# Moving the product that gives a routing position, and its copy, ahead of other work in an attention and mixture-of-experts block

## The chip, the cores and the metric

The kernel runs on one core of a Trainium2 chip. The core has five engines with queues of their own: TensorE (PE, matrix products; its weight loads are shown apart as PEld), VectorE (DVE), ScalarE (ACT), GpSimd (POOL) and SyncE (SP, which here only issues DMAs). Each engine works through its instructions in order and waits on semaphores for the others. The metric is the time of the program on the device in microseconds (us), the median of several runs. Everything is computed in float32.

## The reference

Input x has 4 sequences of 2048 tokens with 256 features, and N = 8192 tokens in all. A conditioning vector gives per sequence six vectors: shift, scale and gate for each of two halves.

```python
h = layernorm(x) * (1 + ca) + sa
x = x + ga * linear_attention(h)      # 16 heads of 16, causal
h = layernorm(x) * (1 + cb) + sb
x = x + gb * moe(h)                   # 8 experts, top 2
```

The attention is linear: queries and keys go through elu(.) + 1, a state S += k v^T runs along the tokens, and each output is (S q) / (z q) with z the running sum of keys. The mixture of experts works with a capacity:

```python
gates = softmax(h @ w_router.T)
topk_gates, topk_idx = top_k(gates, 2)
position_in_expert = cumsum(one_hot(topk_idx).sum(1), axis=0) - 1
keep = position_in_expert < 1280      # ceil(8192 / 8 * 1.25)
y = sum over the kept experts of gate * (silu(h @ w_gate.T) @ w_down[e].T)
```

So a token's place in an expert depends on all the tokens before it.

## The kernel before

Tokens are taken in 16 groups of G = 512, each of four tiles of 128 tokens. A first stage does the attention and the routing of all groups, a second stage (`expert`, line 667) does the eight experts, each on 1280 rows fetched from a table `slots` in DRAM.

In the first stage PE, ACT, DVE and POOL run exactly the order in which the program writes its instructions; nothing reorders them. The main loop (line 767) goes over steps `g` of four parts `j`, and weaves the work of five groups together: the attention of group `g` itself (`scores`, `attend`, `keep_state`, `from_state`, `project_out`), queries, values and denominators of group `nxt` = g+1, the first LayerNorm of `nrm` = g+2, second LayerNorm and router of `prv` = g-1, and the last routing part, `positions` and `dispatch`, of `old` = g-2. Loading is two groups ahead of that. So `positions` is called in 16 steps, g = 2 to 17, of which 13 also have values to compute.

These names are needed to follow the steps, with the lines of the profile:

- `project_out` (L504, L505): `pw` on PE, then DVE adds it to `x`, and the statistics follow (L285).
- `keys_by_token` (L366, L371): `pk` on PE, copied by ACT to `kk`.
- `running_keys` (L381, L386): a DVE scan `zc`, then a POOL product `qs`.
- `values` (L346, L354): `pv` on PE in two halves, each copied by ACT to `vpad` in two copies.
- `normalise` (L306): four ACT scalings, to `xna` for the first LayerNorm and to `hrow` for the second. `second_norm` (L516, L517) has POOL first fill columns of `hrow` with the sequence's modulation (four copies, only in steps with g%4 of 1 or 2).
- `positions` (L582, L585, L589): two products into one bank `pp`, a running count within the group (`tri` times `mask`) and the counts before it (`ones` times `cnt`), 128x32 each, then an ACT copy to `pos`. `mask` and `cnt` come from `ranks` (L566, L575) one step earlier.
- `dispatch` (L604 to L626): 14 small DVE operations from `pos` to the slot numbers `idx`, and the gate weights in `hrow`. The rows themselves are sent by POOL's indirect DMAs (`send`, L641) in parts j=2 and j=3.
- `scores` (L430, L436): `psc` on PE, and two DVE operations that mask it into `at`. `denominators` (L394, L399, L401): `pd` on PE, `den` and `rden` on DVE. `to_features` (L318, L319): four transposes `pta` or `ptm` on PE, an ACT scaling to `hTa` or `hTm`, twice each. `scaled_q` (L412, L417, L419): `pr` on PE, then DVE and ACT.
- `keep_state` (L451, L460, L461, L463): `pst` on PE, `s_add` on ACT, `s_acc` and `s_msk` on POOL.

PSUM has 8 banks. Four hold `psc`, one each `po` and `pst`, and only two are left for all tiles taken with `bank(...)`: `pk`, `pw`, `pv`, `pp`, `pd`, `pta`, `ptm`, `pr`, `pl`, `lt`, `pq`. A tile that takes one of the two banks has to wait until the tile before it in the same bank has been read. Which of the two a tile gets is decided when the program is built.

Of the kernel before, what the change touches and what calls it, by code (L numbers as in the profile page):

```python
# [66 lines left out]
def adaln_block(ctx: ExitStack, tc, x, wqkvT, woutT, wrT, wgT, wdT, cT, wmod, out):  # L67
# [8 lines left out]
    def bank(name):  # L76
        return ps.tile([P, 512], F32, tag="bank", name=name)
# [5 lines left out]
    def load_x(g):  # L83
        xs[g] = xpool.tile([P, NT, D], F32, tag="x", name=f"x_{g}")
        nc.sync.dma_start(xs[g], xg[g])
# [169 lines left out]
    def sums(g):  # L255

        xn = G_["xna", g] = w1.tile([P, NT, D], F32, tag="xna", name=f"xna_{g}")
        sm = small.tile([P, NT], F32, tag="suma", name=f"suma_{g}")
        for j in range(NT):
            nc.scalar.activation(xn[:, j, :], xs[g][:, j, :], AF.Identity, accum_out=sm[:, j : j + 1])  # L260
        nm = small.tile([P, NT], F32, tag="nma", name=f"nma_{g}")
        nc.gpsimd.tensor_scalar(nm, sm, -1.0 / D, None, ALU.mult)
        G_["nm"] = nm

    def squares(g):

        xn, nm = G_["xna", g], G_.pop("nm")
        sq = small.tile([P, NT], F32, tag="sqa", name=f"sqa_{g}")
        for j in range(NT):
            nc.scalar.activation(  # L270
                xn[:, j, :], xs[g][:, j, :], AF.Square, bias=nm[:, j : j + 1], accum_out=sq[:, j : j + 1]
            )
        ve = small.tile([P, NT], F32, tag="vea", name=f"vea_{g}")
        nc.gpsimd.tensor_scalar(ve, sq, 1.0 / D, LN_EPS, ALU.mult, ALU.add)
        rstd = small.tile([P, NT], F32, tag="rstda", name=f"rstda_{g}")
        nc.gpsimd.tensor_tensor(rstd, ve, mhalf, ALU.pow)
        nmr = small.tile([P, NT], F32, tag="nmra", name=f"nmra_{g}")
        nc.gpsimd.tensor_tensor(nmr, nm, rstd, ALU.mult)
        G_["ns", "a"] = nmr, rstd
# [22 lines left out]
    def normalise(g, which, src, dst):  # L302

        nmr, rstd = G_.pop(("ns", which))
        for j in range(NT):
            nc.scalar.activation(  # L306
                dst[:, j, :], src[:, j, :], AF.Identity, bias=nmr[:, j : j + 1], scale=rstd[:, j : j + 1]
            )

    def to_features(g, which, m):  # L310

        b = g // GPB
        xn = G_.pop(("xna", g)) if which == "a" else hrows[g % 2]
        hT = w1.tile([P, NH, G], F32, tag=f"hT{which}", name=f"hT{which}_{g}")
        for h in range(NH):
            pt = bank(f"pt{which}_{g}_{h}")
            for j in range(NT):
                nc.tensor.transpose(pt[:, j * P : (j + 1) * P], xn[:, j, h * P : (h + 1) * P], ident)  # L318
            nc.scalar.activation(  # L319
                hT[:, h, :], pt, AF.Identity,  # L320
                bias=modc[:, m, h, b : b + 1], scale=modc[:, m + 1, h, b : b + 1],
            )
        G_[f"hT{which}", g] = hT
# [255 lines left out]
    def positions(g):  # L579
        gt_, mask, rank, cnt = G_["route", g]  # L580
        pp = G_["pp"] = bank(f"pp_{g}")
        nc.tensor.matmul(  # L582
            pp[:, : NT * NE], tri, mask.rearrange("p j e -> p (j e)"), start=True, stop=False
        )
        nc.tensor.matmul(  # L585
            pp[:, : NT * NE], ones, cnt[:, :NT, :].rearrange("p j e -> p (j e)"), start=False, stop=True
        )
        pos = small.tile([P, NT * NE], F32, tag="pos", name=f"pos_{g}")
        nc.scalar.copy(pos, pp[:, : NT * NE])  # L589
        G_["pos"] = pos  # L590
# [38 lines left out]
    def free_slots(i, then):  # L629

        for e in range(NE):
            at = e * CAP + i * P
            init = nc.sync.dma_start(slots[at : at + P, :], free)
            apart(init, "to_slots", join=False)
            after(init, [then])
# [104 lines left out]
    with tc.manual_schedule(engines={ET.PE, ET.Activation, ET.DVE, ET.Pool}):  # L740
        for g in range(2):
            sums(g)
            squares(g)
            normalise(g, "a", xs[g], G_["xna", g])
            to_features(g, "a", 0)
            for h in range(NH):
                first_k = project(g, "k", h, D, 2)
            if g == 0:
                load_x(2)
                for i in range(2):  # L750
                    free_slots(i, first_k)
                for h in range(NH):
                    project(0, "q", h, 0, 1)
                running_keys(0, (0, 1))
                values(0, 0)
                values(0, 2)
                denominators(0)
                keys_by_token(0)
                scaled_q(0)
                gated_out(0)  # L760
            else:
                for i in range(2, 4):
                    free_slots(i, first_k)
        sums(2)

        last = None
        for s in range((NG + 2) * NT):
            g, j = divmod(s, NT)
            nxt = g + 1 if g + 1 < NG else None
            nrm = g + 2 if g + 2 < NG else None  # L770
            far = g + 3 if g + 3 < NG else None
            prv = g - 1 if 0 <= g - 1 < NG else None
            old = g - 2 if g >= 2 else None

            def done(last=last):
                if last is not None:
                    project_out(*last)
                    if last[1] == NT - 1:
                        added.append(nc.sync.dma_start(og[last[0]], xs[last[0]]))

            if g < NG:
                masked = scores(g, j)
                if s % 2 == 1 and 4 + s // 2 < TPE:
                    free_slots(4 + s // 2, masked)
            if last is not None:
                attend(*last)
            if nxt is not None and j == 2:
                denominators(nxt)
            if prv is not None and j == 3:
                logits(prv)  # L790
            if g < NG and not (g % GPB == GPB - 1 and j == NT - 1):
                keep_state(g, j)
            for i in {2: (0, 1), 3: (2, 3)}.get(j, ()):
                if old is not None:
                    send(old, i)
            if j == 0:
                if nxt is not None:
                    project(nxt, "q", 0, 0, 1)
                done()
                if prv is not None:  # L800
                    spread_of(prv)
                if nxt is not None:
                    project(nxt, "q", 1, 0, 1)
                    running_keys(nxt, (0,))
                if nrm is not None:
                    squares(nrm)
            elif j == 1:
                if nxt is not None:
                    keys_by_token(nxt)
                done()  # L810
                if nxt is not None:
                    running_keys(nxt, (1,))
                    values(nxt, 0)
                    values(nxt, 2)
                if nrm is not None:
                    normalise(nrm, "a", xs[nrm], G_["xna", nrm])
                if prv is not None:
                    second_norm(prv)
                if old is not None:
                    positions(old)  # L820
                    dispatch(old)
                if far is not None:
                    load_x(far)
            elif j == 2:
                if nrm is not None:
                    to_features(nrm, "a", 0)
                done()
                if prv is not None:
                    to_features(prv, "m", 2)
                if nxt is not None:  # L830
                    scaled_q(nxt)
            else:
                if nrm is not None:
                    project(nrm, "k", 0, D, 2)
                done()
                if nrm is not None:
                    project(nrm, "k", 1, D, 2)
                if g % GPB == GPB - 1 and g + 1 < NG:
                    gated_out(g // GPB + 1)
                if far is not None:  # L840
                    sums(far)
                if prv is not None:
                    ranks(prv)
            last = None
            if g < NG:
                from_state(g, j)
                G_["s_old"] = G_.get("s_new")
                last = (g, j)
# [51 lines left out]
```

## Time and profile before

| | us |
|---|---|
| median of 9 runs | 1149.13 (1144.88 to 1158.18) |
| the profiled execution | 1149.41 |
| its span in the profile | 1147.7 |
| from one `pos` copy to the next in the middle of the loop (263.35 to 307.75) | 44.4 |
| first `pos` copy, last `pos` copy | 168.9, 781.0 |

Busy time over the span: PE 945.3 (82%), DVE 621.6 (54%), POOL 560.0 (49%), ACT 441.9 (39%). PE is busy longest, but this share is an average, and the granted TensorE clock moves between full and half speed during the run (mean 0.899).

A line of the timeline has the start in us from the span's start, the duration in us, the engine, the line of the kernel, the operation, output and inputs, shapes, how many instructions are merged into it, and in brackets the idle time of the engine just before with what ended it. A line of the waits has who waited for whom, total us, how many times, and the longest. A line of the stretches has the stretch, its length, the busy time of the engines with the number of records, the granted clock, the DMA share and GB/s.

### The profile page before, as it was taken

How to read it: one execution, taken by the hardware profiler on the slowest of the kernel's cores; microseconds unless marked ns; L12 is line 12 of the kernel's file. 1: busy time of each engine (PE TensorE's matmuls, PEld its weight loads, DVE VectorE, ACT ScalarE, POOL GpSimd, SP SyncE). 2: the span in 40 equal slices, each digit the busy share in tenths (PEclk: the TensorE clock that was granted, in tenths of full speed). 3: DMA queues.
4: the chain of work that ended last, by engine and by line, in shares of the span. 5: the costliest groups of instructions: out<-in, count | busy, mean ns of one | idle time of the engine just before them, and what ended most of it. 6: DMA issues, size and time to landing. Idle time of an engine off the chain costs nothing. (4 is left out here: it accounts for less than half of the span.)

```text
span 1147.7 us, 18139 instructions
## 1 busy us (share of the span) xinstructions
PE 945.3 (82%) x6832; PEld 668.7 (58%) x6832; DVE 621.6 (54%) x1244; ACT 441.9 (39%) x1054; POOL 560.0 (49%) x738
## 2 busy tenths in 40 slices
PE   6759988698898887888888988740899999888996
PEld 5437665465566666666656656520567556556664
DVE  3326566464764665665665566642655555544553
ACT  0456664455554545544545533210222222121221
POOL 3023561744645545645635646634535455454463
PEclk9889998798988989988988988875899999988998
DMA  5179977433232342331221110122665656555531
GB/s 183 49 271 387 369 300 258 157 122 127 101 144 93 112 167 93 112 134 68 76 101 70 46 48 29 45 77 79 258 227 189 217 199 217 180 189 180 199 120 55
DMA packets 71096, 173.61 MB, mean 151 GB/s; under 512 B 13664, under 2 KB 34400, under 8 KB 71008
## 3 DMA queue, kind: packets, MB, share of 16 engines
q1 hardware_dynamic: 39040, 101.66, 24.6%
q0 software_dynamic: 26112, 63.45, 15.0%
q10 hardware_dynamic: 5856, 7.35, 2.0%
q8 instruction: 53, 0.87, 0.3%
q14 instruction: 35, 0.29, 0.1%
HBM read 68.66 MB, written 129.20 MB: 172 GB/s over the span
## 5 line engine op out<-in xcount | busy, mean ns | idle before, releaser
L714 PE MATMUL pe<-wd,hid 128*128 128x256 f32 x640 | 162.5, 393 | 18.3 <-DVE y L721 8.1
L641 POOL DMA_INDIRECT slots<-hrow,idx x128 | 130.6, 1021 | 82.5 <-issue 34.0
L436 DVE TENSOR_TENSOR at<-psc,tri 128x1024 f32<-128x1024 f32 x128 | 150.1, 1214 | 28.5 <-PE psc L430 28.5
L714 PEld LDWEIGHTS pe<-wd,hid 128*128 128x128 f32 x640 | 118.4, 193 | 66.9 <-DVE y L721 25.6
L700 PE MATMUL ph<-hTe,wg_sb 128*128 128x512 f32 (+1 forms) x384 | 155.3, 530 | 1.2 <-ACT hTe L695 0.9
L726 POOL DMA_INDIRECT out_dram<-y,tok x80 | 84.1, 1051 | 104.5 <-issue 38.5
L708 ACT ACTIVATE th<-ph 128x512 f32<-128x512 f32 (+1 forms) x96 | 50.5, 526 | 196.6 <-PE ph L700 170.1
L675 POOL DMA_INDIRECT xc<-out_dram,tok x80 | 84.6, 1057 | 72.5 <-issue 43.0
L461 POOL TENSOR_TENSOR s_acc<-s_acc,s_add 128x256 f32<-128x256 f32 x56 | 45.7, 816 | 126.0 <-ACT s_add L460 119.8
L504 PE MATMUL pw<-wob,oT 128*128 128x256 f32 x256 | 79.5, 439 | 27.7 <-ACT hTa L319 11.5
L700 PEld LDWEIGHTS ph<-hTe,wg_sb 128*128 128x128 f32 x384 | 71.6, 193 | 43.7 <-issue 32.7
L709 DVE SCALAR_TENSOR_TENSOR hid<-th,ph 128x512 f32<-128x512 f32 (+1 forms) x96 | 57.2, 596 | 49.0 <-ACT th L708 40.2
L721 DVE SCALAR_TENSOR_TENSOR y<-pe,rows 128x256 f32<-128x256 f32 x80 | 38.6, 482 | 82.3 <-PE pe L714 61.4
L504 PEld LDWEIGHTS pw<-wob,oT 128*128 128x128 f32 x256 | 50.4, 209 | 53.3 <-issue 16.6
L483 PE MATMUL po<-at,vpad 128*32 128x128 f32 x2048 | 73.2, 276 | 3.5 <-issue 3.5
L430 PE MATMUL psc<-qeo,k 32*128 32x256 f32 x1024 | 75.2, 408 | 0.1
L483 PEld LDWEIGHTS po<-at,vpad 128*32 128x32 f32 x2048 | 54.0, 109 | 27.1 <-issue 26.7
L338 DVE SCALAR_TENSOR_TENSOR k<-exk,k 128x512 f32<-128x512 f32 x32 | 22.2, 692 | 87.1 <-ACT k L337 85.4
L332 PE MATMUL pk<-hTa,wqkv_sb 128*128 128x512 f32 x128 | 64.6, 631 | 4.4 <-ACT k L337 4.4
L318 PE MATMUL ptm<-ident,hrow 128*128 128x128 f32 x128 | 33.9, 412 | 39.7 <-DVE den L399 23.2
L332 PE MATMUL pq<-hTa,wqkv_sb 128*128 128x512 f32 x128 | 61.3, 604 | 5.1 <-ACT q L337 5.1
L346 PE MATMUL pv<-wqkv_sb,hTa 128*128 128x256 f32 x256 | 58.5, 382 | 0.0
(153 smaller groups left out, 1694.0 us busy)
## 6 DMA issues: line engine op xcount, KB each, us to landing
slots<-free SPq DMA_DIRECT2D x80, 518.0 KB, 6.8
rows<-slots SPq DMA_DIRECT2D x16, 2072.0 KB
rows<-slots SPq DMA_DIRECT2D x8, 1036.0 KB
x<-in_x_dram SPq DMA_DIRECT2D x16, 512.0 KB, 4.0
out_dram<-x SPq DMA_DIRECT2D x16, 512.0 KB, 6.4
wd<-in_wdT_dram ACTq DMA_DIRECT2D x8, 512.0 KB, 3.8
slots<-hrow,idx POOLq DMA_INDIRECT x128
wmod_sb<-in_wmod_dram ACTq DMA_DIRECT2D x1, 1536.0 KB
```

The costliest lines, as they stand in the source:

```text
L332: nc.tensor.matmul(pq, wqkv_sb[:, k, o + h * P : o + (h + 1) * P], hT[:, k, :], start=(k == 0), stop=(k == NH - 1))
L346: nc.tensor.matmul(pv[:, i * D : (i + 1) * D], hT[:, k, (j + i) * P : (j + i + 1) * P], wqkv_sb[:, k, 2 * D : 3 * D], start=(k == 0), stop ...
L430: nc.tensor.matmul(psc[:, a, h], kT[r : r + 32, h, cols], qeo[r : r + 32, h, :, cols], start=True, stop=True,)
L436: masked = nc.vector.tensor_tensor(at, psc[:, 2 * m : 2 * m + 2].rearrange("p i h q t -> p (i h q) t"), tri.unsqueeze(1).to_broadcast([P, ...
L483: nc.tensor.matmul(po[32 * a : 32 * a + 32, h * P : (h + 1) * P], vp[:, j, h * 4 + a, q : q + 2, :], att[a // 2][:, a % 2, h, q, :], start ...
L504: nc.tensor.matmul(pw[:, :D], oT[:, h, :], wob[:, h, :], start=(h == 0), stop=(h == NH - 1))
L641: row = nc.gpsimd.indirect_dma_start(out=slots[:, :], out_offset=bass.IndirectOffsetOnAxis(ap=idx[:, c, j : j + 1], axis=0), in_=hr[:, j, ...
L675: got = nc.gpsimd.indirect_dma_start(out=xc[:, i + j, :], out_offset=None, in_=out[:, :], in_offset=bass.IndirectOffsetOnAxis(ap=tok[:, j ...
L700: nc.tensor.matmul(ph[:, :m], wg_sb[:, k, f * P : (f + 1) * P], hT[:, k, :m], start=(k == 0), stop=(k == NH - 1),)
L709: nc.vector.scalar_tensor_tensor(hid[:, f, :m], th[:, :m], 1.0, ph[:, :m], ALU.add, ALU.mult)
L714: nc.tensor.matmul(pe[:, j, :], hid[:, f, j * P : (j + 1) * P], wds[e][:, f, :], start=(f == 0), stop=(f == NF - 1),)
L726: put = nc.gpsimd.indirect_dma_start(out=out[:, :], out_offset=bass.IndirectOffsetOnAxis(ap=tok[:, j : j + 1], axis=0), in_=y[:, j, :], in ...
```

## The change

In part j=1 of each step, `positions(old)` is called right after `done()` (which runs `project_out`), ahead of the second `running_keys`, the `values` of the next group and both LayerNorm scalings. `dispatch(old)` stays where it was. What is computed is unchanged.

```diff
                 if nxt is not None:
                     keys_by_token(nxt)
                 done()
+                if old is not None:
+                    positions(old)
                 if nxt is not None:
                     running_keys(nxt, (1,))
                     values(nxt, 0)
@@
                 if prv is not None:
                     second_norm(prv)
                 if old is not None:
-                    positions(old)
                     dispatch(old)
                 if far is not None:
                     load_x(far)
```

## The prediction

> **What bounds the kernel now.** I read the page first (span, clock), then the table of waits, then the timeline of one loop step, then stretches of the timeline against each other.
>
> ```profile
> span 1147.7 us, 18139 instructions
> ...
> DVE slot L604 <- ACT pos L589: 91.4, 16, 9.4
> ...
> PE ptm L318 <- DVE den L399: 23.2, 13, 4.3
> ```
>
> DVE's costliest wait is for `pos`: 16 times, 91.4 us. What matters is who queues behind it. The timeline of step g=8 shows that (start, duration, engine, line; in brackets the idle time before it and its releaser):
>
> ```profile
> 430.90 1.10 PE L504 MATMUL pw<-wob,oT 128*128 128x256 f32 x4 [0.57 <-ACT kk L371]
> ...
> 439.97 0.17 ACT L589 COPY pos<-pp 128x32 f32<-128x32 f32 x1
> ...
> 440.17 0.18 DVE L604 TENSOR_SCALAR slot<-pos 128x32 f32<-128x32 f32 x1 [6.00 <-ACT pos L589]
> 440.19 0.66 PE L318 MATMUL pta<-ident,xna 128*128 128x128 f32 x4 [0.68 <-ACT pos L589]
> ...
> 443.57 2.35 DVE L436 TENSOR_TENSOR at<-psc,tri 128x1024 f32<-128x1024 f32 x2
> ...
> 446.17 0.66 PE L318 MATMUL ptm<-ident,hrow 128*128 128x128 f32 x4 [1.80 <-DVE den L399]
> ```
>
> `pp` was done on PE at 435.82; its copy waited on ACT behind the value copies and eight scalings (436.02 to 440.06). DVE had been free since its scan ended at 434.17. Then 14 small `dispatch` operations (3.4 us), two masks and `den` ran in a row, and PE idled 0.68 + 0.87 + 0.87 + 1.80 + 0.87 = 5.1 us between `pst` and `pr`. The wait is on PE's path.
>
> A yardstick: step g=1 has the same work but no positions, dispatch or sends (stretch, length, PE busy, records, clock, DMA share, GB/s).
>
> ```profile
> 123.90:159.80 35.90, 33.62 (x345) 1.00 0.90 331
> 263.40:307.80 44.40, 38.02 (x349) 0.88 0.31 121
> ```
>
> 345 against 349 records (four are `pp`): 35.9 us at full clock, 44.4 us at 0.88. The clock, around the stall of g=9 (busy PE, PEld, DVE, ACT, POOL, then the clock):
>
> ```profile
> 482.30:485.70 3.40, 1.31 (x8) 0.84 (x8) 2.36 (x10) 2.44 (x7) 1.88 (x4) 1.00 0.40 108
> 485.70:489.10 3.40, 2.07 (x4) 1.17 (x4) 3.26 (x9) 0.24 (x1) 1.78 (x2) 0.50 0.26 96
> ```
>
> Of stretches of this length, laid on the clock's own steps, each at full clock with PE busy 49% or less is followed by half clock; one with 52% (441.3 to 444.7) is not. Half clock then lasts 10.2 us in nearly every step: `pr` takes 3.62 us there (g=10) and 2.05 in g=1.
>
> **The change part by part.** Nothing is added or removed: four `pp` matmuls and one copy move in each of 16 steps, 13 of which have values. DVE, POOL, SP and all DMAs keep their order.
>
> *PE.* `pp` now stands before the values. `cnt` (425.45) and its bank (freed by `kk`, 431.24) are long ready. As the program is built, `pp` and the first half of `pv` share a PSUM bank, so `pv` waits for the copy: it starts not at 431.84 but after 0.53 of `pp` (435.29 to 435.82), 0.17 of copy and twice 0.05 between engines, 0.8 later. `pp`'s old place gives back 0.2. Bounds: 0 (if later stalls hide it) and 0.8; I take 0.8, being nearest to g=1, which has no stall to hide it.
>
> *ACT.* `pos` costs 0.17 in either place. The rest of ACT is 0.8 late with `pv`: scalings end 440.86, `oT` and `s_add` follow, the first `hTa` ends 442.13 (was 441.66), the second 442.83 (was 443.19).
>
> *Banks.* The later banks change hands too: the second `pta` waits for `den` (as in g=1) and no longer for the first `hTa`; `pw` for the first `hTa`; the `ptm` pair for the second `hTa` and the addition at L505.
>
> *DVE.* `pos` is there at 432.6, so dispatch starts at the scan's end, 434.17, not 440.17. But there it meets POOL's `s_acc`, `s_msk`, `qs`, and in steps with g%4 of 1 or 2 also four row copies (L516, 0.78 each). What that does is seen in g=2:
>
> ```profile
> 170.56 0.73 POOL L461 TENSOR_TENSOR s_acc<-s_acc,s_add 128x256 f32<-128x256 f32 x1
> 170.57 0.76 DVE L609 SCALAR_TENSOR_TENSOR keep<-pos,mask 128x32 f32<-128x32 f32 x1
> ...
> 171.36 0.72 POOL L463 TENSOR_TENSOR s_msk<-s_acc,bd 128x256 f32<-128x256 f32 x1
> 171.36 0.76 DVE L612 TENSOR_TENSOR gates<-gates,keep 128x32 f32<-128x32 f32 x1
> ```
>
> A 0.19 us operation lasts until POOL's is over, and the next loses the race again: one DVE operation per POOL operation (reductions are not held: L614 took 0.19 at 441.17, inside `s_acc`). This speaks against the change. [...]
>
> So the steps fall into two kinds.
>
> *Steps without the row copies (g=3, 4, 7, 8, 11, 12).* In g=8 five operations fit before `s_acc` (435.23), the rest go one by one past three POOL operations: masks at about 439.0, 0.8 after `psc` allows, against 443.57. `den` ends 441.5, second `pta` 442.2, `pw` 442.2, `ptm` 443.2 and 443.95, `pr` 444.73, against 448.24: 3.5 earlier. PE's idle pieces shrink to under 0.9 us, so no stretch falls below 70% busy and the clock stays full. Then a step is g=1's 35.94 (`pw` to `pw`) + 0.8 + 0.2 for slack = 36.95 against 44.4: 7.4 saved. Five such steps 37, and g=8, which had little half clock (42.7 to the next), 5.7. Sum 43.
>
> *Steps with them (g=5, 6, 9, 10, 13).* In g=9 `s_acc` holds POOL from the scan's end (476.85) to 477.37, then `s_msk`, `qs` and the copies run to 482.48. With one operation past each, dispatch ends near 483.5 instead of 486.6. `den` follows at 486.0, and the second `pta`, which now needs it, comes at 486.1 where it was 484.5. `pr` starts at 489.4 against 492.1. But PE idles 2.5 us in one piece (483.6 to 486.1); a 3.4 us stretch around it is under 49% in about three of four positions, so half clock is likelier and takes back about 1. Per step: 4.7 at full clock, 1.5 at half; I take 2. Sum 10. Bounds: 0 (half clock earlier than before) and 7.4 (POOL holds nothing).
>
> *The ends.* g=2: the slot resets that hold its last sends start when a mask ends, which is 7 earlier, and the POOL wait for them (12.4) stays: 6.5. g=14: dispatch again behind POOL, masks about 9.9 after `pw` where they came at 11.15: 1.3. g=15: DVE waited only 0.58: 0.5. g=16: `pos` came at 764.08 behind four scalings and could come at 760.5, so the POOL sends start 3.5 earlier: 3.5. g=17 waits for POOL's `cnt`: 0. Sum 12.
>
> *Sum.* 43 + 10 + 12 = 65 us. The profiled execution took 1149.41 (span 1147.70 and 1.71 around it), 0.28 over the median of 1149.13: 1149.4 - 65 = 1084 us. The expert stage merely starts earlier.
>
> **The rivals.**
>
> *POOL does not hold DVE there, or the clock stays full everywhere.* Then g=5, 6, 9, 10, 13 save up to 7.4 too, 27 more: 1057 us. [...] The trace differs: in 482.3 to 485.7 no gap exceeds 0.9 us, PE is 39% busy, and half clock follows. By the trace's own rows full clock in these steps needs a lucky position: (4.7 - 2) x 5 = 13 less, 1071 us.
>
> *More is held than I think.* If POOL's `rstda` holds DVE too (434.17 to 435.0 in g=8), masks come near 440.1, `den` 442.65, and PE idles 2.0 us before the second `pta`: the first kind of step gets half clock as well and saves about 4, the second kind 1: 23 + 5 + 12 = 40, 1109 us.
>
> *Slower: the values wait and dispatch gains nothing.* The 0.8 us in 13 steps is 10 us paid for sure on PE. If the masks came no earlier than before (12.7 us after `pw`), this remained: 1160 us. It decides if DVE is held to that point in all steps; POOL's train ends at most 8.9 us after `pw`, which speaks against it, and the second `pta` now needing `den` speaks for a loss where dispatch is late.
>
> *The move does nothing*, because `pp` waits for `cnt` or DVE for something else: 1149 us. `cnt` is ready 6 us ahead of `pw`'s end, so I give it little.
>
> **How the numbers follow.** Forecast (1084, between 1070 and 1098) 0.47; less contention or clock loss (1050 to 1070) 0.23; more held (1098 to 1125) 0.20; nothing or nearly (1143 to 1155) 0.04; slower 0.06. About 0.5% (6 us) is what a measurement of this kernel can tell from no change. Range 1052 to 1118, leaving out 0.10 above and a little at either end of the cases. Faster 0.90, same 0.04, slower 0.06.
>
> **What would show it.** Right: the wait of L604 for `pos` falls from 91.4 to about 15 (g=17 keeps 9.4); a new wait `pv` for `pos` of 0.3 to 0.8; `ptm` no longer waits for `den`, the second `pta` does, longest where L516 runs; steps of 37 us and of 42 us side by side; in the latter dispatch operations of 0.7 to 1.3 us; half clock only in the latter. Wrong: steps all alike, half clock gone everywhere or still everywhere, or a late `qs` on POOL that holds `pd`.

## The result, and the profile after

The changed kernel takes 1101.25 us in the median of 10 runs (1098.41 to 1109.44), the kernel before 1149.26 in 31 runs beside it: a ratio of 0.9598, with a 95% interval of 0.9572 to 0.9624. That is 48 us, or 4.0%; 65 us had been forecast. The profiled execution took 1098.38 us, with a span of 1096.7, against 1149.41 and 1147.70 before, so the two traces differ by 51.0 us. The mean granted clock rose from 0.899 to 0.935. Here and below a ratio is that of mean times without each kernel's first, profiled execution and without slow ones more than 1.5% above its fastest, so it can differ a little from the quotient of the two medians.

The waits of the changed kernel from 160 to 760 us (who waited, for whom; total, times, longest, in us):

```profile
ACT oT L491 <- remote: 27.2, 4, 9.6
...
PE pta L318 <- DVE den L399: 21.1, 11, 3.5
...
DVE at L436 <- remote: 14.6, 3, 5.6
...
PE po L483 <- issue: 9.3, 17, 1.0
...
DVE slot L604 <- ACT pos L589: 5.4, 1, 5.4
...
PEld pv L346 <- ACT pos L589: 5.0, 13, 0.4
```

DVE's wait for `pos` has fallen from 91.4 us to 5.4, which is g=17 alone. In its place stand the wait of the second `pta` for `den`, and 0.4 us of `pv` behind `pos` in 13 steps. But the list also has waits that nobody had forecast: `oT` and the masks wait long for something that the profile can name no local releaser for ("remote"), and the short matmuls of `po` for "issue". Before the change `oT` had two such waits (13.7 us, in steps 14 and 15), the masks none, and `po` nine of at most 0.5 us (3.5 in all). These waits lead to the missing 14 us.

The timeline shows what the change was to do, in g=8, the step that the prediction worked out (start, duration, engine, line; in brackets the idle time before it):

```profile
413.68 1.10 PE L504 MATMUL pw<-wob,oT 128*128 128x256 f32 x4 [0.58 <-ACT kk L371]
...
415.18 0.18 ACT L589 COPY pos<-pp 128x32 f32<-128x32 f32 x1 [1.16 <-PE pp L585]
...
415.42 3.72 PE L346 MATMUL pv<-wqkv_sb,hTa 128*128 128x256 f32 x16 [0.28 <-ACT pos L589]
...
416.86 0.16 DVE L604 TENSOR_SCALAR slot<-pos 128x32 f32<-128x32 f32 x1
...
421.59 2.35 DVE L436 TENSOR_TENSOR at<-psc,tri 128x1024 f32<-128x1024 f32 x2
...
424.20 0.66 PE L318 MATMUL pta<-ident,xna 128*128 128x128 f32 x4 [1.01 <-DVE den L399]
...
427.45 2.05 PE L412 MATMUL pr<-rden,spread 128*128 128x128 f32 x16
```

`slot` starts with no wait at all, 3.2 us after `pw` where it was 9.3, and `pr` comes 13.8 us after `pw` at full clock (2.05 us; 1.00 granted in the whole step).

A step with the four row copies, g=9:

```profile
455.65 0.64 DVE L604 TENSOR_SCALAR slot<-pos 128x32 f32<-128x32 f32 x1
...
456.32 1.20 DVE L605 TENSOR_TENSOR slot<-slot,pos 128x32 f32<-128x32 f32 x1
...
457.42 3.12 POOL L516 COPY hrow<-modr 128x768 f32<-128x768 f32 x4
...
462.08 2.35 DVE L436 TENSOR_TENSOR at<-psc,tri 128x1024 f32<-128x1024 f32 x2
...
464.69 0.66 PE L318 MATMUL pta<-ident,xna 128*128 128x128 f32 x4 [3.22 <-DVE den L399]
```

POOL holds DVE's 0.19 us operations for up to 1.20 us; the masks start 10.15 us after `pw` (451.93) and PE idles 3.22 us for `den`.

Where did the gain go? I measure each step from its copy `pos` to the next one's (L589 in the timeline). This table has the lengths in us for the kernels whose steps are compared below; single steps of the others are given where they are needed. "Starving" and "free" are explained in the next part.

| kernel | g=3 | 4 | 5 | 6 | 7 | 8 | 9 | 10 | 11 | 12 | 13 | 15 |
|---|---|---|---|---|---|---|---|---|---|---|---|---|
| before | 43.2 | 44.4 | 44.5 | 44.3 | 43.4 | 42.7 | 44.1 | 44.3 | 43.8 | 44.5 | 42.2 | 28.4 |
| changed, profiled beside it | 45.9 | 38.0 | 38.8 | 39.8 | 43.9 | 38.3 | 40.7 | 40.8 | 44.0 | 38.1 | 40.5 | 26.3 |
| `changed_third` (starving) | 45.1 | 38.0 | 39.2 | 40.3 | 44.4 | 38.2 | 40.2 | 39.9 | 43.8 | 38.0 | 38.6 | 26.3 |
| `sends_apart_2` (starving) | 40.3 | 39.6 | 38.9 | 40.3 | 39.2 | 41.1 | 39.4 | 40.8 | 39.8 | 40.6 | 38.5 | 19.0 |
| `apart_and_copies` (starving) | 43.3 | 39.7 | 38.0 | 38.0 | 39.7 | 40.8 | 38.1 | 38.1 | 39.6 | 40.9 | 37.7 | 19.0 |
| `dispatch_late` (starving) | 44.3 | 42.8 | 42.0 | 40.4 | 40.7 | 41.6 | 40.4 | 42.0 | 40.9 | 42.9 | 41.9 | 21.0 |
| `copies_late` (free) | 37.8 | 36.8 | 36.8 | 37.9 | 37.4 | 36.8 | 37.0 | 37.9 | 37.9 | 36.8 | 37.0 | 19.6 |
| `short_rows` (free) | 37.8 | 36.8 | 36.9 | 38.6 | 36.4 | 36.8 | 37.7 | 37.6 | 36.5 | 36.8 | 36.9 | 19.9 |
| `pos_behind_values` (free) | 36.8 | 39.3 | 42.6 | 42.5 | 39.2 | 39.4 | 42.6 | 42.6 | 40.8 | 39.7 | 42.9 | 17.4 |

There are three kinds of step, not two. Steps 4, 8 and 12 fell to 38; steps 5, 6, 9, 10 and 13 to about 40; steps 3, 7 and 11 did not fall at all. The last three have no `keep_state` in j=3, so POOL issues all eight sends without a pause. In g=7 the timeline of the changed kernel shows PE beside this train:

```profile
385.94 1.15 PE L430 MATMUL psc<-qeo,k 32*128 32x256 f32 x16
...
387.38 0.97 POOL L641 DMA_INDIRECT slots<-hrow,idx  x1 [0.31 <-issue]
...
389.38 0.43 PE L483 MATMUL po<-at,vpad 128*32 128x128 f32 x4 [1.02 <-issue]
...
390.81 0.66 PE L483 MATMUL po<-at,vpad 128*32 128x128 f32 x4 [1.00 <-issue]
...
390.85 2.36 DVE L436 TENSOR_TENSOR at<-psc,tri 128x1024 f32<-128x1024 f32 x2 [4.50 <-remote]
...
392.25 0.64 PE L526 MATMUL pl<-hTm,wr 128*32 128x128 f32 x3 [0.34 <-issue]
...
393.98 0.37 ACT L491 COPY oT<-po 128x256 f32<-128x256 f32 x1 [5.92 <-remote]
```

`po` has 32 matmuls that take 1.08 us in other steps. Here, after the first 24, groups of four start 1.43 us apart, while PE waits for nothing that the profile shows. The masks start 3.8 us after the records of `psc` have ended (387.09), `oT` 2.5 us after those of `po`. I call this a starved stretch. From 393.67 on PE has its matmuls in a row again, 1.5 us after POOL issued the last send (392.15 is its end) and before the rows have all been moved (their packets end near 395.2).

Before the change POOL had issued the whole train of g=7 (400.88 to 410.9) when the `po` of `attend` began (411.54); by moving `idx` forward against PE's work the change brought issuing and `attend` together. Rows on their way are not enough to starve PE: before the change they were still moving beside `psc`, `po` and `pl`, and PE was busy all the time (busy PE, PEld, DVE, ACT, POOL, then the clock, the DMA share and GB/s):

```profile
410.00:412.00 2.00, 2.00 (x35) 1.40 (x34) 0.41 (x1) 1.41 (x3) 1.99 (x3) 0.85 0.99 387
412.00:414.00 2.00, 2.00 (x42) 1.33 (x35) 1.66 (x2) 0.64 (x2) 0.34 (x1) 1.00 0.92 359
```

### The profile page after: what moved, and what is told of

Same layout as the page of the kernel before. It is cut to its first block, busy times and chain, and to the rows that moved or that the text cites. A ratio compares the mean times of both kernels' runs of the same rounds, so it can differ in the third digit from the quotient of the medians.

```text
span 1096.7 us, 18137 instructions
## 1 busy us (share of the span) xinstructions
PE 920.9 (84%) x6832; PEld 644.5 (59%) x6832; DVE 644.8 (59%) x1244; ACT 439.6 (40%) x1054; POOL 554.3 (51%) x738
## 5 line engine op out<-in xcount | busy, mean ns | idle before, releaser
L726 POOL DMA_INDIRECT out_dram<-y,tok x80 | 82.7, 1033 | 102.4 <-issue 37.9
L700 PEld LDWEIGHTS ph<-hTe,wg_sb 128*128 128x128 f32 x384 | 71.9, 194 | 44.4 <-issue 33.6
L504 PE MATMUL pw<-wob,oT 128*128 128x256 f32 x256 | 73.9, 414 | 24.5 <-ACT kk L371 12.0
L461 POOL TENSOR_TENSOR s_acc<-s_acc,s_add 128x256 f32<-128x256 f32 x56 | 42.5, 760 | 99.1 <-ACT s_add L460 95.8
L483 PE MATMUL po<-at,vpad 128*32 128x128 f32 x2048 | 79.0, 279 | 9.6 <-issue 9.3
L721 DVE SCALAR_TENSOR_TENSOR y<-pe,rows 128x256 f32<-128x256 f32 x80 | 38.6, 483 | 80.5 <-PE pe L714 56.5
L504 PEld LDWEIGHTS pw<-wob,oT 128*128 128x128 f32 x256 | 48.1, 200 | 49.3 <-issue 16.9
L332 PE MATMUL pk<-hTa,wqkv_sb 128*128 128x512 f32 x128 | 68.9, 668 | 4.2 <-ACT k L337 4.1
L346 PE MATMUL pv<-wqkv_sb,hTa 128*128 128x256 f32 x256 | 61.2, 393 | 3.6 <-ACT pos L589 3.6
L695 ACT COPY hTe<-pte 128x512 f32<-128x512 f32 (+1 forms) x48 | 24.2, 515 | 80.8 <-PE pte L694 76.3
```

What stands on the lines that cost most here:

```text
L332: nc.tensor.matmul(pq, wqkv_sb[:, k, o + h * P : o + (h + 1) * P], hT[:, k, :], start=(k == 0), stop=(k == NH - 1))
L346: nc.tensor.matmul(pv[:, i * D : (i + 1) * D], hT[:, k, (j + i) * P : (j + i + 1) * P], wqkv_sb[:, k, 2 * D : 3 * D], start=(k == 0), stop ...
L483: nc.tensor.matmul(po[32 * a : 32 * a + 32, h * P : (h + 1) * P], vp[:, j, h * 4 + a, q : q + 2, :], att[a // 2][:, a % 2, h, q, :], start ...
L504: nc.tensor.matmul(pw[:, :D], oT[:, h, :], wob[:, h, :], start=(h == 0), stop=(h == NH - 1))
L700: nc.tensor.matmul(ph[:, :m], wg_sb[:, k, f * P : (f + 1) * P], hT[:, k, :m], start=(k == 0), stop=(k == NH - 1),)
L726: put = nc.gpsimd.indirect_dma_start(out=out[:, :], out_offset=bass.IndirectOffsetOnAxis(ap=tok[:, j : j + 1], axis=0), in_=y[:, j, :], in ...
```

## The experiments

My theory after the result: the bank cost and the earlier dispatch are as forecast, POOL's row copies explain the steps of 40 us, and the train of eight sends the steps of 44. One fact has to be said first. The kernel before took 1131 us on two occasions (the first four experiments and the last) and 1144 to 1149 on the three others. On the 1131 occasions no kernel shows starved stretches, on the others every changed kernel has some, and the kernel before has one in step 15 (and single gaps of 0.3 to 0.5 us in `po` in nine other steps). I call the occasions free and starving, compare times within an occasion, and compare across them only step lengths. The record names the chip for four of the five occasions, and it is another one each time: 6 and 10 were free, 14 and 5 starving. So a difference between occasions may be one between chips.

**Sends apart.** In steps with g%4 = 3 the last four sends move behind `ranks`:

```diff
-            for i in {2: (0, 1), 3: (2, 3)}.get(j, ()):
+            apart8 = g % GPB == GPB - 1 and g < NG
+            for i in {2: (0, 1), 3: () if apart8 else (2, 3)}.get(j, ()):
...
                 if prv is not None:
                     ranks(prv)
+                if old is not None and apart8:
+                    send(old, 2)
+                    send(old, 3)
```

> Edit: in steps with g%4 = 3 the last four of the eight sends move from the start of j=3 to its end, behind `ranks`; all else as in the changed kernel. Theory (in steps 3, 7, 11 and 15 POOL issues eight sends in a row, and while their rows move PE gets its short `po` and `pl` matmuls only four at a time): the issue gaps at L483 and L526 go, steps 7 and 11 fall from 43.9 and 44.0 us to the 38.2 of steps 4, 8 and 12, step 3 from 45.9 to about 40, and step 15 loses some 3 to 5. Together 17 to 22 us: 1080 to 1085 us against 1101. Rival (PE's gaps come from the clock or from PE's own order, and the sends only happen to be there): the gaps stay, 1097 to 1105 us. Second rival (four sends later in the step hold POOL's next additions and give it back): gaps gone, but 1090 to 1100.

Measured, on a free occasion: 1057.07 us against 1130.99, a ratio of 0.9358 (0.9298 to 0.9418). Steps 7 and 11 took 36.4 and 36.5. This looked like the theory proved, but the next three experiments, on the same occasion, spoiled that.

**Row copies late.** The four copies L516 leave `second_norm` for a function of their own, called behind `ranks`:

```diff
-        if g % GPB < 2:
-            for j in range(NT):
-                nc.gpsimd.tensor_copy(hr[:, j, D : 4 * D], ...)
...
                     ranks(prv)
+                    fixed_rows(prv)
```

> Edit: the four row copies L516 of steps with g%4 = 1 or 2 move from j=1 to the end of j=3, behind `ranks`. Theory (POOL's work beside `dispatch` holds DVE's operations one by one, the row copies most): steps 5, 6, 9, 10 and 13 fall from 38.8, 39.8, 40.7, 40.8 and 40.5 us to 37.5 to 38.2; about 11 us together, less up to 3 for what the copies hold at their new place: 1090 to 1093 us. Rival (these steps are long because the second `pta` waits for `den` whatever POOL does): masks and `den` come as late as now, 1098 to 1104 us.

Measured: 1057.83 us, a ratio of 0.9351 (0.9317 to 0.9384); steps 5, 6, 9, 10 and 13 took 36.8 to 37.9. But this kernel keeps the train of eight, and its steps 3, 7 and 11 were 37.4 to 37.9 as well. Its timeline in g=7, answering to the one above:

```profile
376.48 1.15 PE L430 MATMUL psc<-qeo,k 32*128 32x256 f32 x16
...
377.42 0.97 POOL L645 DMA_INDIRECT slots<-hrow,idx  x1 [0.30 <-issue]
377.56 1.08 PE L483 MATMUL po<-at,vpad 128*32 128x128 f32 x32
377.69 2.35 DVE L436 TENSOR_TENSOR at<-psc,tri 128x1024 f32<-128x1024 f32 x2 [0.80 <-PE psc L430]
...
378.76 0.37 ACT L491 COPY oT<-po 128x256 f32<-128x256 f32 x1 [0.16 <-PE po L483]
```

The train runs at the same rhythm (0.97 us each, 0.30 between), its rows move about as fast (379 to 383 GB/s from 377 to 385 us, where the starving trace has 356 to 396), it begins 5.4 us ahead of `po` (372.20) where it was 4.8 (382.18), and PE does not starve. The row copies themselves gave less than the 11 us expected: `sends_apart` beside it has them at their old place, and its steps 5, 6, 9, 10 and 13 are only 3.2 us longer together.

**Eight sends in every step.** Doubling the suspected cause:

```diff
-            for i in {2: (0, 1), 3: (2, 3)}.get(j, ()):
+            for i in {3: (0, 1, 2, 3)}.get(j, ()):
```

> Edit: in every step all eight sends are issued in j=3, in one row; now only steps 3, 7, 11 and 15 have eight in a row. Theory (a row of eight starves PE's short matmuls): issue gaps at L483 in nearly every step, in the `attend` that runs some 5 us behind the first send, 4 to 6 us each in nine or ten more steps: 1135 to 1155 us. Rival (the number in a row does not matter): 1097 to 1108 us, gaps at most in the steps that have them now.

Measured: 1058.32 us, a ratio of 0.9346 (0.9312 to 0.9379), with every step from 4 to 13 at 36.5 to 37.1. The rival was right: on this occasion a train of eight costs nothing. Its steps with row copies take 37.0 though the copies stand at their old place in POOL's order. In g=9 POOL gets to the first of them at 441.43, when `idx` (439.75) is done, so they hold nothing of `dispatch`.

**Positions behind the values.** One half of the change: ahead of the scalings on ACT, but behind the values again.

```diff
-                if old is not None:
-                    positions(old)
                 if nxt is not None:
                     running_keys(nxt, (1,))
                     values(nxt, 0)
                     values(nxt, 2)
+                if old is not None:
+                    positions(old)
```

> Edit: `positions` goes behind the values again, but stays ahead of the LayerNorm scalings on ACT: one half of the change alone. Theory (the gain is dispatch's earlier start; the bank that `pp` shares with `pv` costs PE 0.3 to 0.8 us a step): `pv` starts some 0.6 us earlier, `pos` comes 4 to 5 us later, behind the value copies, DVE waits 2.5 to 3 us for it at the scan's end, and the 13 steps get 1 to 2 us longer each net of the bank: 1114 to 1128 us. Rival (the bank costs as much as the earlier start gives): 1095 to 1105 us. Second rival (only the scalings mattered, any place ahead of them does as well, and without the bank wait): 1090 to 1097.

Measured: 1095.21 us, a ratio of 0.9669 (0.9634 to 0.9704), 38 us more than `sends_apart` beside it (the changed kernel itself was not run on this occasion). Its times in us are those of a free occasion, so the expectation's 1114 to 1128 has to be read as a distance: 13 to 27 above the changed kernel. The direction was right and the loss larger. The timeline of g=8:

```profile
411.81 1.10 PE L504 MATMUL pw<-wob,oT 128*128 128x256 f32 x4 [0.58 <-ACT kk L371]
...
416.94 0.20 ACT L589 COPY pos<-pp 128x32 f32<-128x32 f32 x1
417.17 0.54 DVE L604 TENSOR_SCALAR slot<-pos 128x32 f32<-128x32 f32 x1 [2.10 <-ACT pos L589]
...
424.04 0.66 PE L318 MATMUL pta<-ident,xna 128*128 128x128 f32 x4 [3.18 <-DVE den L399]
```

`pos` comes 5.1 us after `pw` instead of 1.5, DVE waits 2.1 us, and the second `pta` 3.18. From step 4 on, steps without row copies take 39.2 to 40.8 us where the other kernels of free occasions take 36.4 to 37.9, steps with them 42.5 to 42.9 where `short_rows` takes 36.9 to 38.6. So the place ahead of the values is worth 2 to 6 us a step, many times what the shared bank costs.

**The changed kernel itself, once more.** The free occasion made it necessary to know what the changed kernel does beside its variants. No edit.

> Edit: none; the changed kernel itself, beside the kernel before on one chip, because the kernel before took 1131 us beside the first four experiments and 1149 us earlier. Theory (the starved stretches of steps 3, 7, 11 and 15 depend on the chip and not on the kernel: `copies_late` keeps the row of eight sends and shows none): where the kernel before takes about 1131, these steps take 37 to 38.5 us and the kernel 1058 to 1068, a ratio near 0.94. Rival (they belong to this kernel's exact timing): 43.9 us again, 1080 to 1090 us, a ratio near 0.96.

> Edit: none; the changed kernel beside the next two on one chip. It has starved stretches so far on two occasions where the kernel before takes 1144 to 1149 us. Theory (the chip decides): where the kernel before takes near 1131, steps 3, 7 and 11 take 37 to 38.5 us here and the kernel 1058 to 1068 (ratio near 0.94); where it takes 1143 to 1150, 43 to 47 us and 1097 to 1104 again. Rival (the experiments with whole steps removed the starved stretches each by its own edit): 43 to 47 us on any chip, a ratio of 0.955 to 0.96.

Both fell on starving occasions: 1100.58 us against 1144.07, a ratio of 0.9555 (0.9513 to 0.9598), and 1108.38 against 1147.95, 0.9647 (0.9602 to 0.9691). Steps 3, 7 and 11 took 47.1, 43.7, 43.8 and 45.1, 44.4, 43.8 us. They could not decide whether the changed kernel itself is free of them where the kernel before takes 1131; that it is, is likely from `copies_late`, `eight_in_every_step` and `short_rows`, which keep its trains of eight.

**The kernel before, once more.** No edit.

> Edit: none; one look at the kernel before on this chip, to see which of its steps are shorter where it takes less than 1149 us. Theory (only the starved stretch of step 15 and the like differ): steps 3 to 13 keep 42 to 44.5 us, and the difference lies in step 15 and in the expert stage. Rival (the chip runs all stages faster): every step is shorter by the same 1.5%.

One run, 1141.42 us, beside the 1144 runs: steps 3 to 13 took 41.6 to 44.3 us, as before. It fell on a starving occasion and so says nothing on what is shorter at 1131; that stays open.

**A bank of its own.** `pp` goes to the bank of `pst`, and `pv` need not wait for `pos`:

```diff
-        pp = G_["pp"] = bank(f"pp_{g}")
+        pp = G_["pp"] = ps_st.tile([P, 512], F32, tag="pst", name=f"pp_{g}")
```

> Edit: the changed kernel with `pp` in the bank of `pst`, so that `pv` no longer waits for the copy `pos`. Theory (the shared bank costs PE its 0.28 us of idle time and the turn of the banks, about 0.4 us in each of 13 steps): 4 to 6 us faster than the changed kernel of this call. Rival (later stalls hide it): within 2 us of it.

Measured: 1096.46 us, a ratio of 0.9563 (0.9528 to 0.9598), beside the changed kernel's 0.9555: no difference. The wait of `pv` for `pos` is gone, and steps 4, 8 and 12 are 37.4 instead of 37.7, 37.9 and 37.9 in `changed_again`, so 0.3 to 0.6 us each. The steps with row copies (40.8, 41.0, 40.1, 39.8, 41.1) did not gain: PE's wait for `den` grew from 17.6 to 22.9 us between 250 and 640 us, as it must if `den` comes no earlier and PE gets there sooner. The 4 to 6 us of the theory did not come; its mechanism shows in the steps without row copies, and the rival's in the others.

**Dispatch late.** If the masks stand behind `dispatch`, why not move `dispatch` behind `den`?

```diff
             elif j == 2:
                 if nrm is not None:
                     to_features(nrm, "a", 0)
+                if old is not None and g < NG:
+                    dispatch(old)
                 done()
```

Up to step 15, two pairs of sends then go to j=3 and two behind `ranks`.

> Edit: the changed kernel with `dispatch` moved behind `den` in j=2 (up to step 15), two of its four `send` pairs in j=3 and two behind `ranks`. Theory (what is left of PE's wait for `den` is the masks standing behind `dispatch`, which POOL holds): the second `pta` no longer waits for `den`, the steps with row copies fall to the 37 us of the others; 5 to 12 us faster than the changed kernel of this call where that shows steps of 39 to 40. Rival (sends so late hold POOL's `rstda` and the additions): same or up to 10 us slower.

Measured: 1108.61 us, a ratio of 0.9666 (0.9624 to 0.9707), slower than the changed kernel's 0.9555 beside it. PE's waits from 250 to 640 us, first of `changed_again`:

```profile
PE pta L318 <- DVE den L399: 17.6, 10, 2.5
...
PE pw L504 <- ACT kk L371: 3.4, 10, 0.6
```

then of `dispatch_late`:

```profile
PE pw L504 <- ACT hTa L319: 10.1, 10, 1.0
PE ptm L318 <- ACT hTm L319: 8.7, 10, 0.9
PE pw L504 <- ACT kk L371: 8.4, 9, 1.8
PE pr L412 <- DVE x L505: 5.9, 10, 1.2
...
PE pta L318 <- DVE den L399: 0.3, 2, 0.2
```

The wait that the theory named is gone (17.6 to 0.3), but the steps with row copies take 40.4 to 42.0 us and not 37, for four others took its place. With `pta` early, PE runs into its two banks instead: each of `pw`, `ptm` and `pr` now waits for ACT or DVE to empty the bank before it. `dispatch` stands ahead of L505 on DVE, which `pr` needs. Of the steps in the table only 3, 7, 11 and 15 gained (47.1, 43.7, 43.8 and 25.4 to 44.3, 40.7, 40.9 and 21.0), the four that had the train of eight.

**Sends apart, where it starves.** The same edit as the first, now on a starving occasion, beside `changed_third`.

> Edit: as `sends_apart`. Theory (eight sends in a row starve PE where the chip does so): on a chip where the changed kernel has starved stretches, steps 3, 7 and 11 fall to 37 to 40 us and step 15 by 4 to 6, together 17 to 22 us under the changed kernel of this call; on a chip where it has none, 0 to 5 us. Rival (spacing the sends does nothing to it; only the chip does): within 4 us of the changed kernel on either.

Measured: 1089.93 us, a ratio of 0.9461 (0.9412 to 0.951), against 1108.38 and 0.9647 for the changed kernel beside it. Steps 3, 7, 11 and 15 get 4.8, 5.2, 4.1 and 7.3 us shorter: spacing the train does help where PE starves. But steps 4, 8, 12 and 16 get 1.6, 2.9, 2.6 and 4.5 longer, so that the last `pos` comes only 9.2 us earlier (725.57 against 734.78). The traces differ by 13.9 us; the other 4.7 lie behind the last `pos`, in a stretch that varies from 362.0 to 370.3 us between the three traces of the changed kernel. Part of the starving has only moved, as g=8 of `sends_apart_2` shows:

```profile
404.26 0.96 POOL L641 DMA_INDIRECT slots<-hrow,idx  x1 [0.30 <-issue]
404.61 0.65 PE L366 MATMUL pk<-ident,k 128*128 128x128 f32 x4 [0.28 <-issue]
...
406.05 0.38 PE L366 MATMUL pk<-ident,k 128*128 128x128 f32 x2 [0.80 <-issue]
...
409.54 6.60 PE L346 MATMUL pv<-wqkv_sb,hTa 128*128 128x256 f32 x16 [0.28 <-ACT pos L589]
```

Now the transposes `pk` come in groups 1.4 us apart beside the delayed sends, though these are only four (400.33 to 405.22), and `pv` behind it takes 6.60 us instead of 3.72. ACT waits 3.87 and 2.17 us for its halves where 2.08 and 1.08 are usual; from these lengths it is estimated to run mostly at half clock.

**Both.** Sends apart and row copies late together, on the same occasion.

> Edit: both, the last four sends of steps with g%4 = 3 behind `ranks` and the row copies L516 at the end of j=3. Theory (two separate losses: the starved stretches, and POOL's copies that hold `dispatch` and so the masks and `den`): the row copies give 1 to 3 us in each of steps 5, 6, 9, 10 and 13 on top of `sends_apart_2`, 5 to 12 us together; all steps from 4 to 13 between 36.7 and 38 us. Rival (the copies are as much in the way at their new place): within 3 us of `sends_apart_2`.

Measured: 1085.40 us, a ratio of 0.9449 (0.9406 to 0.9491). Steps 5, 6, 9, 10 and 13 are 0.9, 2.3, 1.3, 2.6 and 0.7 us shorter than in `sends_apart_2`, 7.9 together and within the 5 to 12 expected; but steps 4, 7, 8, 11 and 12 stay at 39.6 to 40.9 us, where all were to be at 36.7 to 38. Step 3 is 2.9 longer, for a reason that stays open. The wait of the second `pta`, first in `sends_apart_2`, then here:

```profile
PE pta L318 <- DVE den L399: 17.9, 10, 2.9
```

```profile
PE pta L318 <- DVE den L399: 9.3, 9, 1.5
```

The last `pos` comes at 718.64, 6.9 us earlier, and the medians differ by 4.5, which their intervals do not separate. It is the fastest version measured on a starving occasion, 23 us below the changed kernel beside it.

**Short rows.** To tell the bytes that the sends move from the act of issuing them, the eight sends of steps 3, 7, 11 and 15 carried a quarter of each row, to another buffer. The tokens of these groups so never reach the expert stage, and only step lengths can be compared.

```diff
-                out=slots[:, :],
+                out=(short if g % GPB == 1 else slots)[:, :],
...
-                in_=hr[:, j, :],
+                in_=hr[:, j, :D] if g % GPB == 1 else hr[:, j, :],
```

> Edit: the changed kernel, but the eight sends of steps 3, 7, 11 and 15 carry only the first 256 numbers of each row (1 KB where it was 4.1 KB), to a buffer of their own; same number of sends, rows and issues, a quarter of the bytes. The tokens of these four groups so never reach the expert stage, which has fewer rows to gather and put back; only the step lengths are to be compared. Theory (the bytes that the sends move starve PE): on a chip where the changed kernel has starved stretches, steps 7 and 11 fall from 43.7 to 44.4 us to about 38, and the gaps at L483 and L526 go. Rival (the issuing itself, the number of rows or the events that each send raises): 43 to 45 us as before. Where the kernel before takes near 1131 us, 37 to 38 us by either, and nothing is told apart.

Measured, one run each: 1053.67 us, the kernel before 1131.04: a free occasion, so nothing is told apart, as the expectation said. Its untouched steps show one thing. They are the changed kernel's own, with the row copies at their old place, and take 36.8 us without copies and 36.9 to 38.6 with them.

**What stays open: why PE starves on one occasion and not on another.** The same program (`sends_apart` and `sends_apart_2`), the same train and about the same transfer rate gave both. The chip is one difference that no run took away: no program was run free and starving on one chip. The traces differ in one more respect. The table of transfers gives no time from issue to landing for the sends on starving occasions (`changed_third`):

```profile
slots<-hrow,idx POOLq DMA_INDIRECT x128
```

and does on free ones (`copies_late`):

```profile
slots<-hrow,idx POOLq DMA_INDIRECT x128, 3.4
```

The starving traces hold 4834 to 5319 landing events, the free ones 6948 to 6973, for some 71110 packets each (68037 in `short_rows`); so the starving traces lack records of events. In the same traces PE's shortest matmuls (`po`, 32 in 1.08 us) stopped in equal groups, and DVE and ACT started late on its results (3.8 us after `psc` and 2.5 us after `po` in g=7); whether that and the lacking events belong together, no run shows. Every run here has a span and a clock, so every one was recorded in some way, and a time without a recorder is not among them.

## Why the prediction was right or wrong, step by step

**What bounded the kernel, and the direction: right.** DVE's wait for `pos` stood on PE's path. It went from 91.4 to 5.4 us (about 15 was expected), and the step lengths followed.

**The PE term, 0.8 us for the shared bank: right in size, too dear in effect.** `pv` starts 1.74 us after `pw` instead of 0.94, exactly the 0.8. `own_bank` shows that of it 0.3 to 0.6 reaches the end in steps without row copies and nothing in the others.

**The first kind of step: right in g=4, 8 and 12, wrong in g=3, 7 and 11.** The chain worked out for g=8 came within 0.2 us but for the second `pta`, which came 0.8 earlier. In us from the start of `pw`:

| | forecast | measured |
|---|---|---|
| masks start | 8.1 | 7.9 |
| `den` ends | 10.6 | 10.5 |
| second `pta` starts | 11.3 | 10.5 |
| `pr` starts | 13.8 | 13.8 |

The step was to be 36.95 and is 38.3; where nothing starves such steps take 36.8. Steps 4, 8 and 12 saved 17.2 us where 20.5 was forecast. But "without the row copies" put steps with and without `keep_state` in j=3 into one class. Steps 3, 7 and 11 were priced at 7.4 each and gained -2.7, -0.5 and -0.2: 25.6 us short, the largest miss. The working costed DVE's and POOL's operations in j=1 and j=2, and did not ask what the sends, which came earlier too, would now run beside. The trace of before had the sign: in its step 15 `pl` already came in groups beside the same train (747 to 752 us), a wait marked "issue" that was not followed up.

**The second kind: too pessimistic.** 2 us each was taken, between bounds of 0 and 7.4. They saved 5.7, 4.6, 3.4, 3.5 and 1.7, together 18.9 instead of 10. The mechanism was right: dispatch operations of 0.64 to 1.20 us in g=9, PE idle 3.22 us before the second `pta` (2.5 forecast), and the wait falls when the copies leave (`apart_and_copies`). What failed was the price of half clock, not its likelihood: it came in four of the five, as "likelier" says, but these four (6, 9, 10 and 13) saved 4.6, 3.4, 3.5 and 1.7 where 1.5 had been put, and step 5, without it, 5.7 where 4.7 had been put.

**Half clock: right in the second kind, missed in the starved steps.** It was to be found in the second kind only. It follows the stall in g=6, 9, 10 and 13, not in g=5, and lasts one stretch of 3.4 us (0.50 or 0.51 granted) where it had lasted 10.2. It also follows the starved stretches of steps 3, 7 and 11, for 6.8. The stretches ahead of it in the changed kernel (busy PE, PEld, DVE, ACT, POOL, then the clock):

```profile
462.20:465.60 3.40, 0.92 (x6) 0.88 (x7) 3.37 (x4) 1.25 (x4) 2.56 (x3) 1.00 0.53 154
387.20:390.60 3.40, 1.52 (x28) 0.81 (x21) 0.00 (x0) 0.86 (x2) 2.61 (x3) 1.00 0.96 380
```

PE is busy 27% and 45% of them, and both are followed by half clock (0.51 and 0.50 in the next 3.4 us), so the forecast's bound of 49% held in these two. The second has no gap longer than 1.02 us: half clock followed a stretch of short gaps, as it did after 482.3 to 485.7 before the change, where none exceeds 0.9 us.

**The ends: 18.3 us instead of 12.** All that the first `pos`, steps 2 and 14 to 16, and the stretch behind the last `pos` give (7.2, 4.2, 0.2, 2.1, -0.1 and 4.7). So g=2 was priced too low (6.5 for the first two), and g=14 and g=16 too high (1.3 and 3.5). The last, 4.7, is no larger than that stretch's own spread from run to run, and is not a gain of the change.

**The sum.** 64.7 forecast, rounded to 65; steps 3, 7 and 11 take 25.6 off it, steps 4, 8 and 12 another 3.3, the second kind adds 8.9 and the ends 6.3: 51.0, as the traces have it. That 1101 us lies in the stated range of 1052 to 1118 is in part luck: the first kind saved 28.9 us less than forecast and the rest 15.2 us more, 4.7 of it in a stretch that varies by itself, and the two cancelled in part. The time fell outside the forecast's own band of 1070 to 1098.

**The rivals.** "Full clock everywhere" (1057) was wrong on the occasion of the result; on a free one it describes the steps well (36.4 to 39.0, in variants of the changed kernel), though even there 3.4 us of half clock remain in a step or two (g=6 of `short_rows`, 38.6 us, and g=5 and 13 of `sends_apart`, 39.0 and 38.7 us). "More is held" (1109) came near in time, for another reason: POOL's `rstda` held no operation of `dispatch` in g=8 (five started inside it, 0.16 to 0.19 us each), and the loss was on PE. "The values wait and dispatch gains nothing" is refuted by `pos_behind_values`: the earlier place saves 2 to 6 us a step, and by `own_bank` the wait costs at most 0.6.

## What to carry to other kernels

When a step is moved forward, everything it releases comes forward as well, transfers included: look up what they will run beside, not only whether they are in order. Class the steps of a loop by all their exceptions (here a skipped `keep_state`) before one price is given to a class, and follow up each "issue" or "remote" wait in the trace, however small. Measure variants beside the changed kernel on one occasion: three variants all near 0.935 looked like three improvements and were mostly one better occasion.

## What the runs showed of the hardware

- On some occasions PE's short matmuls stopped in groups of at most four, 1.43 us apart (some 0.72), for 5 to 8 us, beside a train of eight indirect sends (4.1 KB rows, 10 us of issues, 356 to 396 GB/s); on others the same train stopped nothing. Beside four sends `pk` stopped for about 2 us (`sends_apart_2`), and eight sends' rows still on their way at 359 to 387 GB/s did not stop PE (g=7 before the change). What in it stops PE was not found.
- DVE's small operations are held by POOL's only where the two meet (0.64 to 1.20 us instead of 0.16 to 0.19): the same row copies cost a step up to 2.6 us (`apart_and_copies` against `sends_apart_2`) or next to nothing (37.0 against 36.8 in `eight_in_every_step`), by whether POOL reaches them before or after `dispatch`.
- With two banks that rotate, taking away one wait (17.6 us) brought four others (33.1 us together, of which two had stood at 3.4 and 0.9).
